# The first two graphs of a pre-norm attention kernel: read by whole rows and turned by the tensor engine, with the first products made one graph at a time

## The chip, the cores and the metric

The kernel runs on one core of a Trainium2 chip. Its time is the device time of one execution in microseconds (us); of five executions the median is 2914.31 us (2913.82 to 2919.03). The profile is of one more execution. Its engines are called PE (tensor engine, matmuls), PEld (its weight loads), DVE (vector), ACT (scalar), POOL (GpSimd) and SP (which here only issues transfers). "ACTq" and "SPq" are transfers being issued by ACT and SP.

## The reference

128 graphs of 128 nodes with 768 features each, all in float32. Each graph is normalised, goes through one attention layer of 12 heads of 64, masked by its adjacency, and the result is added to the input.

```python
h = jnp.maximum(_layernorm(x, axis=-1), 0.0)          # x: (128, 128, 768)
q, k, v = (split_heads(h @ W + b) for W, b in ((Wq, bq), (Wk, bk), (Wv, bv)))
scores = einsum('bhqd,bhkd->bhqk', q, k) / sqrt(64) + beta * adj[:, None]
scores = where(adj[:, None] > 0, scores, -9e15)
out = x + merge_heads(einsum('bhqk,bhkd->bhqd', softmax(scores), v))
```

## The kernel before, in words

**Groups and slices.** The graphs are taken in 32 groups of four (`NG` = 32). The projection of a group is cut into three slices of the weights: `qk0` (q and k of heads 0 to 5), `v`, and `qk1` (q and k of heads 6 to 11). A slice is a product of a 2 x 3 block matrix A and a 3 x 3 block matrix B. A is the group's normalised input, transposed: block `A{r}{k}` has graphs 2r and 2r+1 (256 columns) and features of chunk k (two sub-blocks of 128). B is the slice's weights, nine blocks of 128 x 2 x 256.

**Two ways of making a slice.** `slice_of` makes it with 15 products instead of 18 (`PRODUCTS`), from sums of blocks of A (`SUMS_A`, 11 DVE adds, line 285) and of B (`SUMS_B`, 15 DVE adds, lines 204 and 207); each product is 4 matmuls, each issued in two halves of 64 columns (line 331). The very first slice, `qk0` of group 0, is made by `plain_slice` (line 466): 6 outputs (r, j), each the sum over k of A{r}{k} times B{k}{j}, so 18 products of 4 matmuls of 256 columns (line 477), which need no sums. A finished output is copied from its PSUM bank by ACT with the bias added (line 484). The `v` and `qk1` slices of group 0 are already made with sums, and the weights of `qk0` are summed for group 1. `sum_weights` overwrites some raw blocks (`HOME`).

**The start.** `load_x` reads a graph with four transfers of 96 KB, one for each quarter of the features, 32 nodes to 32 partitions, so that 32 x 32 block transposes on DVE (line 279) finish the transpose. As a node's features then lie on four partitions, its mean and variance need a sum across partitions: `stats` (DVE, line 227), `moments_1` and `moments_2` (small matmuls with `mean8`, lines 238 and 254, and short DVE operations), a power on POOL (line 261), and `norm` on ACT (line 272), before `to_hT` transposes. Four graphs are loaded first, on the SP and ACT queues in turn (line 154), then the weights of `qk0` on SP, and `beta` and two biases on ACT (lines 211, 216, 217). `half(0, ...)` (line 498) makes the A blocks of graphs 0 and 1; `half(1, ...)` those of graphs 2 and 3, with its moments placed after steps 1 and 2 of the plain slice. Ten matmuls on the identity (line 526) run between the moments and the first product.

**What sets the order.** Each engine runs its instructions in order. A scheduler orders them from the order of the code; `tc.issue_after` holds an instruction back behind another. Extra work is hung on the steps of a slice (`then(n, f)`, run after product n). Transfers share eight completion semaphores in turn, so a transfer is issued only when the one eight before it in the code has landed, and everything behind it on its queue waits, ACT's arithmetic included.

**Further on in group 0.** During the `v` slice DVE takes the statistics of group 1 and the sums of `qk1`; at the end of it `bias_1` and `bias_2` prepare the mask of group 0 (DVE lines 298 to 304, ACT line 305, DVE line 310). Scores of heads 0 to 5 (line 377, `scores(0, 0)`) are made behind the second product of `qk1`; they take six PSUM banks, which DVE frees one by one when it adds the mask (line 381, tile `e`). The same happens with `scores(0, 1)` behind the second product of group 1.

The first matmuls of the plain slice:

```python
for k in range(3):
    a, b = A[G, f"A{r}{k}"], wt[sl, f"B{k}{j}"]
    for i in range(2):
        for c in range(2):
            nc.tensor.matmul(p[:, i, :], b[:, c, i * P:(i + 1) * P], a[:, c, :], ...)
```

Of the kernel before, what the change touches and what calls it, by code (L numbers as in the profile page):

```python
# [10 lines left out]
F32 = mybir.dt.float32  # L11
# [6 lines left out]
P = 128  # L18
HEADS = 12
GRP = 4  # L20
# [74 lines left out]


HOME = {"B00": "T12", "B10": "T10", "B02": "T0", "B20": "T4", "B11": "T13"}
SLICES = ("qk0", "v", "qk1")


SC_AT = 1
AV_AT = (5, 8, 11)

LAST = (0, 1, 2, 3, 5, 7, 6, 10, 11, 9, 4, 12, 8, 13, 14)

# [6 lines left out]
def direct(ctx, tc, x, adj, wq, bq, wk, bk, wv, bv, beta, out, bad):  # L112
# [35 lines left out]
    def load_x(G, g, engines):  # L148
        t = xg[G, g] = work.tile([P, NB, QD], F32, tag="x", name=f"x_{G}_{g}")
        src = x[G * GRP + g].rearrange("(b i) (a f) -> a i b f", i=SQ, a=NB)  # L150
        for a in range(NB):
            engines[a % len(engines)].dma_start(t[a * SQ:(a + 1) * SQ], src[a])  # L152

    for g in range(GRP):
        load_x(0, g, (nc.sync, nc.scalar))
    ident = const.tile([P, P], F32, name="ident")
    make_identity(nc, ident)


    fold = const.tile([P, SQ], F32, name="fold")  # L160
    nc.vector.tensor_reduce(fold, ident.rearrange("p (a i) -> p i a", i=SQ), AX.X, ALU.add)
    mean8 = const.tile([P, NB, SQ], F32, name="mean8")
    made = nc.vector.tensor_scalar(mean8, fold[:, None, :].to_broadcast([P, NB, SQ]), -0.125, None, op0=ALU.mult)
    nhalf = const.tile([P, 1], F32, name="nhalf")
    nc.gpsimd.memset(nhalf, -0.5)
    ones = const.tile([P, 1], F32, name="ones")
# [4 lines left out]
    seen_b = const.tile([P, GRP], F32, name="seen_b")  # L171
    nc.gpsimd.memset(seen_b, 0.0)
    vring = [const.tile([P, 2 * GRP, VE], F32, name=f"v{i}") for i in range(7)]
    for v in vring:
        nc.gpsimd.memset(v[:, :, HD:VE], 1.0)
    nv = [0]


# [10 lines left out]
            for i, w in enumerate((wq, wk)):  # L189
                nc.sync.dma_start(t[:, :, i * P:(i + 1) * P], part(w, oc * P, P))  # L190

    def load_weights(sl):
        for b in [f"B{k}{j}" for j in range(3) for k in range(3)]:
            t = const.tile([P, 2, H2], F32, name=f"{sl}_{HOME.get(b, b)}")
            load_block(sl, int(b[1]), int(b[2]), t)
            wt[sl, b] = t
# [9 lines left out]
        else:  # L206
            nc.vector.tensor_tensor(wt[sl, name], wt[sl, a], wt[sl, b], ALU.add if sign > 0 else ALU.subtract)

    load_weights("qk0")
    beta_c = const.tile([P, 1], F32, name="beta_c")  # L210
    nc.scalar.dma_start(beta_c, beta[None, :].to_broadcast([P, 1]))

    nc.gpsimd.tensor_scalar(beta_c, beta_c, ISCALE, None, op0=ALU.mult)
    bqk = const.tile([P, 2, NC], F32, name="bqk")
    with nc.allow_non_contiguous_dma(reason="two biases of one row each"):
        nc.scalar.dma_start(bqk[:, 0, :], bq.rearrange("(c p) -> p c", p=P))
# [5 lines left out]
    def stats(G, g):  # L222

        if G not in st:
            st[G] = stat.tile([P, GRP * NB, nc.vector.BN_STATS_DIM], F32, tag="st", name=f"st_{G}", bufs=2)
        for b in range(NB):
            nc.vector.bn_stats(st[G][:, g * NB + b, :], xg[G, g][:, b, :])  # L227
# [4 lines left out]
    def moments_1(G, lo, hi):  # L232

        n = hi - lo
        bank = pm[G, lo, "bank"] = take()
        pm[G, lo] = bank[:, 0:4 * n].rearrange("p (s b h) -> p s b h", s=2, h=2)
        for q in range(0, P, HD):
            nc.tensor.matmul(pm[G, lo][q:q + HD, 0], mean8.rearrange("p a i -> p (a i)")[:, q:q + HD],
                             halves(G, lo, hi, 1), start=True, stop=True)
        mean = stat.tile([P, n], F32, tag="mean", name=f"mean_{G}_{lo}", bufs=2)  # L240
        nc.vector.tensor_reduce(mean, pm[G, lo][:, 0], AX.X, ALU.add)
        d = stat.tile([P, n, 2], F32, tag="dev", name=f"dev_{G}_{lo}", bufs=2)
        nc.vector.tensor_tensor(d, halves(G, lo, hi, 1), mean[:, :, None].to_broadcast([P, n, 2]), ALU.add)
        nc.vector.tensor_tensor(d, d, d, ALU.mult)
        nc.vector.scalar_tensor_tensor(d, halves(G, lo, hi, 2), 2.0 / QD, d, op0=ALU.mult, op1=ALU.add)
        return mean, d

    squares = {}

    def moments_2(G, lo, hi, mean, d):  # L250

        n = hi - lo
        for q in range(0, P, HD):
            squares[0] = nc.tensor.matmul(pm[G, lo][q:q + HD, 1], mean8.rearrange("p a i -> p (a i)")[:, q:q + HD],
                                          d, start=True, stop=True)
        ve = stat.tile([P, n], F32, tag="ve", name=f"ve_{G}_{lo}", bufs=2)
        nc.vector.tensor_reduce(ve, pm[G, lo][:, 1], AX.X, ALU.add)
        give(pm[G, lo, "bank"])
        nc.vector.tensor_scalar(ve, ve, -1.0, EPS, op0=ALU.mult, op1=ALU.add)
        r = stat.tile([P, n], F32, tag="rstd", name=f"rstd_{G}_{lo}", bufs=2)  # L260
        nc.gpsimd.tensor_tensor(r, ve, nhalf.to_broadcast([P, n]), ALU.pow)  # L261
        t = stat.tile([P, n], F32, tag="shift", name=f"shift_{G}_{lo}", bufs=2)
        shifted = nc.gpsimd.tensor_tensor(t, mean, r, ALU.mult)  # L263
        for b in range(lo, hi):
            rstd[G, b], shift[G, b] = r[:, b - lo:b - lo + 1], t[:, b - lo:b - lo + 1]
        return shifted

    def norm(G, g):
        for b in range(NB):
            t = xg[G, g][:, b, :]  # L270
            n = g * NB + b
            nc.scalar.activation(t, t, AF.Relu, bias=shift[G, n], scale=rstd[G, n])  # L272
# [193 lines left out]
    def plain_slice(G, sl, todo):  # L466

        n = 0
        for r in range(2):
            for j in range(3):  # L470
                bank = take()
                p = bank.rearrange("p (i w) -> p i w", i=2)
                for k in range(3):
                    a, b = A[G, f"A{r}{k}"], wt[sl, f"B{k}{j}"]
                    for i in range(2):
                        for c in range(2):
                            nc.tensor.matmul(p[:, i, :], b[:, c, i * P:(i + 1) * P], a[:, c, :],  # L477
                                             start=(k == 0 and i == 0 and c == 0), stop=(c == 1),
                                             skip_group_check=True)
                    if k == 2:  # L480
                        t = qk[G, sl, r, j] = work.tile([P, 2, H2], F32, tag="qk", name=f"{sl}_{G}_{r}_{j}", bufs=8)
                        oc = j + 3 * int(sl[2])
                        for i in range(2):
                            nc.scalar.activation(t[:, i, :], p[:, i, :], AF.Identity, bias=bqk[:, i, oc:oc + 1])
                        give(bank)
                    for f in todo.get(n, ()):
                        f()
                    n += 1
# [1 line left out]

    adj_0 = load_adj(0)
    nc.sync.dma_start(bv_b, bv[None, :].to_broadcast([P, D]))
    load_weights("v")

    PARTS = (((0, NB), (NB, 2 * NB)), ((2 * NB, 4 * NB),))
    first = {}

    def half(r, step):
        for lo, hi in PARTS[r]:
            graphs = range(lo // NB, hi // NB)  # L500
            if step == 0:
                for g in graphs:
                    stats(0, g)
            elif step == 1:
                first[lo] = moments_1(0, lo, hi)
            else:
                first["pool"] = moments_2(0, lo, hi, *first[lo])
                for g in graphs:
                    norm(0, g)
        if step == 2:  # L510
            for k in range(3):
                first["dve"] = to_hT(0, r, k)

    def after(f, *args):

        with tc.issue_after(first["dve"].ins), tc.issue_after(first["pool"].ins):
            return f(*args)

    with tc.issue_after(made.ins):
        for step in range(3):  # L520
            half(0, step)

    with tc.issue_after(squares[0].ins):
        warm = take()
        for n in range(10):
            nc.tensor.matmul(warm[:, 0:P], ident, ident, start=True, stop=True)
        give(warm)

    def behind_adds(f, *args):

        with tc.issue_after(added[0].ins):
            return f(*args)

    for G in range(NG):
        todo = attention(G - 1, 1) if G else {}

        def then(n, f):
            todo.setdefault(n, []).append(f)
# [7 lines left out]
                if G:  # L546
                    then(11 + g, lambda g=g: stats(G + 1, g))
        if not G:
            load_weights("qk1")
            with tc.issue_after(first["dve"].ins):  # L550
                half(1, 0)
            then(1, lambda: half(1, 1))
            then(2, lambda: half(1, 2))
            for n in range(len(SUMS_A)):
                then(n + 5, lambda n=n: after(sum_acts, 0, n))
            for n in range(len(SUMS_B)):
                then(n // 2 + 5, lambda n=n: after(sum_weights, "v", n))
            plain_slice(0, "qk0", todo)
        else:
            if G == 1:  # L560
                for n in range(8, len(SUMS_B)):
                    then(n - 8, lambda n=n: sum_weights("qk0", n))
            slice_of(G, "qk0", todo)
        todo = {SC_AT: [lambda: scores(G, 0)]} if G else {}
        if G + 1 < NG:
# [188 lines left out]
```

## Time and profile before

| | us |
|---|---|
| median of five executions | 2914.31 |
| their range | 2913.82 to 2919.03 |
| the profiled execution | 2915.2 |
| its span, first to last instruction | 2913.4 |
| PE busy in the span | 2885.1 (99%) |
| DVE / ACT / POOL busy | 1993.4 / 796.1 / 375.6 |
| first matmul of the plain slice (line 477) | 15.56 |
| first product of the `v` slice (line 331) | 49.37 |

A row of a timeline gives the start, the duration, the engine, the line, what is written and read, the shape and the count, and in brackets how long the engine had been idle and what ended that. PE records a float32 matmul as two entries, so "x8" is one product of four matmuls of 256 columns. In a table by stretches, the column behind the busy times is the granted clock of PE as a share of full speed.

### The profile page before, as it was taken

How to read it: one execution, taken by the hardware profiler on the slowest of the kernel's cores; microseconds unless marked ns; L12 is line 12 of the kernel's file. 1: busy time of each engine (PE TensorE's matmuls, PEld its weight loads, DVE VectorE, ACT ScalarE, POOL GpSimd, SP SyncE). 2: the span in 40 equal slices, each digit the busy share in tenths (PEclk: the TensorE clock that was granted, in tenths of full speed). 3: DMA queues.
4: the chain of work that ended last, by engine and by line, in shares of the span. 5: the costliest groups of instructions: out<-in, count | busy, mean ns of one | idle time of the engine just before them, and what ended most of it. 6: DMA issues, size and time to landing. Idle time of an engine off the chain costs nothing.

```text
span 2913.4 us, 81848 instructions
## 1 busy us (share of the span) xinstructions
PE 2885.1 (99%) x35526; PEld 2022.2 (69%) x35526; DVE 1993.4 (68%) x5155; ACT 796.1 (27%) x1703; POOL 375.6 (13%) x307
## 2 busy tenths in 40 slices
PE   8999999999999999999999999999999999999998
PEld 6666676766767667766677666677667776666766
DVE  7866676766767666767667676677766677666765
ACT  1322222323223232222222232322323222222221
POOL 1111111111111111111111111111111111111110
PEclk9999999999999999999999999999999999999999
DMA  5211122111221212222112212122121222111211
GB/s 162 69 56 45 53 70 65 52 54 44 67 70 52 58 42 61 71 59 56 45 52 70 67 50 55 45 67 70 53 62 37 61 70 59 56 45 49 67 41 38
DMA packets 358622, 172.22 MB, mean 59 GB/s; under 512 B 84464, under 2 KB 358128, under 8 KB 358256
## 3 DMA queue, kind: packets, MB, share of 16 engines
q1 hardware_dynamic: 355392, 166.14, 20.8%
q8 instruction: 280, 4.59, 0.6%
q10 hardware_dynamic: 2864, 0.79, 0.1%
q14 instruction: 86, 0.70, 0.1%
HBM read 116.53 MB, written 50.33 MB: 57 GB/s over the span
## 4 chain that ended last, share of the span: by engine, by line
PE 81%; issue 9%; DVE 5%; POOL 2%; DMA 2%; SPq 1%; ACT 0%; ACTq 0%; POOLq 0%; DVEq 0%
PE bank L331 70%; PE bank L377 5%; PE bank L406 5%; DMA x<-in_x_dram 2%; PE bank L477 1%; POOL rstd L261 1%; DVE S L285 1%; POOL xo L411 1%; DVE qk L356 1%; DVE st L227 1%; DVE A L279 1%; DVE o L392 0%; SPq L152 0%; ACT x L272 0%; DVE v L342 0%
## 5 line engine op out<-in xcount | busy, mean ns | idle before, releaser
L331 PE MATMUL bank<-S,qk_T 128*64 128x256 f32 x7056 | 828.7, 382 | 10.5 <-DVE e L381 8.9
L331 PEld LDWEIGHTS bank<-S,qk_T 128*64 128x64 f32 x7056 | 506.0, 138 | 271.1 <-DVE e L381 13.1
L356 DVE TENSOR_TENSOR qk<-qk,bank 128x512 f32<-128x512 f32 x630 | 430.0, 683 | 348.8 <-PE bank L331 348.4
L352 ACT ACTIVATE qk<-bank,bqk 128x256 f32<-128x256 f32 x756 | 313.0, 470 | 1014.2 <-PE bank L331 859.3
L331 PE MATMUL bank<-A,qk_T 128*64 128x256 f32 x4032 | 478.7, 379 | 0.0
L331 PE MATMUL bank<-S,qk_B 128*64 128x256 f32 x4032 | 478.4, 380 | 0.0
L411 POOL TENSOR_TENSOR xo<-xo,o 128x512 f32<-128x512 f32 x189 | 255.8, 1354 | 1611.1 <-DVE o L392 1030.4
L331 PE MATMUL bank<-v_T,S 128*64 128x256 f32 x3584 | 422.9, 381 | 0.0
L384 ACT ACTIVATE e<-e 128x512 f32<-128x512 f32 x378 | 227.5, 631 | 679.7 <-DVE e L381 679.2
L347 DVE TENSOR_TENSOR v<-v,bank 128x512 f32<-128x512 f32 x320 | 220.0, 688 | 264.8 <-PE bank L331 264.8
L331 PEld LDWEIGHTS bank<-A,qk_T 128*64 128x64 f32 x4032 | 284.2, 137 | 136.5 <-issue 0.2
L331 PEld LDWEIGHTS bank<-S,qk_B 128*64 128x64 f32 x4032 | 278.4, 137 | 127.9 <-DVE qk L356 0.8
L331 PEld LDWEIGHTS bank<-v_T,S 128*64 128x64 f32 x3584 | 252.8, 137 | 125.8 <-issue 5.7
L272 ACT ACTIVATE x<-x,shift,rstd 128x192 f32<-128x192 f32 x512 | 228.0, 533 | 343.7 <-POOL shift L263 343.7
L331 PE MATMUL bank<-v_B,S 128*64 128x256 f32 x2048 | 244.8, 380 | 0.0
L381 DVE SCALAR_TENSOR_TENSOR e<-bank,biasT 128x512 f32<-128x512 f32 x378 | 231.4, 680 | 13.6 <-PE bank L377 13.5
L331 PE MATMUL bank<-v_T,A 128*64 128x256 f32 x2048 | 238.4, 379 | 0.0
L342 DVE TENSOR_TENSOR v<-bv_b,bank 128x512 f32<-128x512 f32 x192 | 131.8, 687 | 145.8 <-PE bank L331 145.8
L406 PEld LDWEIGHTS bank<-v,e 128*64 128x64 f32 x6048 | 208.6, 138 | 27.4
L279 DVE STREAM_TRANSPOSE A<-x 128x256 f32<-128x256 f32 x384 | 215.7, 613 | 7.5 <-ACT x L272 7.4
L227 DVE BATCH_NORM_STATS2 st<-x 128x6 f32<-128x192 f32 x512 | 160.5, 348 | 71.6 <-DMA x<-in_x_dram 71.4
L406 PE MATMUL bank<-v,e 128*64 128x65 f32 x6048 | 208.4, 221 | 0.0
(79 smaller groups left out, 1726.6 us busy)
## 6 DMA issues: line engine op xcount, KB each, us to landing
x<-in_x_dram SPq DMA_DIRECT2D x504, 96.0 KB, 2.3
xo<-in_x_dram SPq DMA_DIRECT2D x189, 256.0 KB, 2.8
out_dram<-xo SPq DMA_DIRECT2D x189, 256.0 KB, 2.2
adj<-in_adj_dram SPq DMA_DIRECT2D x128, 64.0 KB, 2.3
qk_T<-in_L_gnn_Wq_dram SPq DMA_DIRECT2D x10, 128.0 KB, 3.3
qk_T<-in_L_gnn_Wk_dram SPq DMA_DIRECT2D x10, 128.0 KB, 3.1
v_T<-in_L_gnn_Wv_dram SPq DMA_DIRECT2D x5, 256.0 KB, 5.9
qk_B<-in_L_gnn_Wq_dram SPq DMA_DIRECT2D x8, 128.0 KB, 3.0
```

Of the source, the lines that this page charges most:

```text
L227: nc.vector.bn_stats(st[G][:, g * NB + b, :], xg[G, g][:, b, :])
L272: nc.scalar.activation(t, t, AF.Relu, bias=shift[G, n], scale=rstd[G, n])
L279: last = nc.vector.transpose(t[:, :, g * N:(g + 1) * N].rearrange("p c (b i) -> p c b i", i=SQ), src)
L331: nc.tensor.matmul(p[q:q + HD, i, :], lhs[:, q:q + HD], rhs, start=(first and i == 0 and c == 0), stop=(c == 1), skip_group_check=True)
L347: added[G] = nc.vector.tensor_tensor(o, o, got, ALU.add if sign > 0 else ALU.subtract)
L352: nc.scalar.activation(t[:, i, :], p[:, i, :], AF.Identity, bias=bqk[:, i, oc:oc + 1], scale=float(sign))
L356: added[G] = nc.vector.tensor_tensor(t, t, p, ALU.add if sign > 0 else ALU.subtract)
L377: nc.tensor.matmul(ps[oc, i][k:k + HD, g * N:(g + 1) * N], t[r, 1, at][:, k:k + HD], t[r, 0, at], start=True, stop=True)
L381: nc.vector.scalar_tensor_tensor(e, ps[oc, i].rearrange("p (g n) -> p g n", g=GRP), SCORE_CAP * ISCALE, biasT[G], op0=ALU.min, op1=ALU.add)
L384: nc.scalar.activation(e, e, AF.Exp, scale=1.0 / ISCALE)
L406: nc.tensor.matmul(pa[q:q + HD, 2 * g + i, :], es[G, oc, i][:, 2 * r + g, q:q + HD], vt[G, "v", r, h // 4][:, 4 * g + h % 4, :], start=Tru ...
L411: nc.gpsimd.tensor_add(t, t, o.rearrange("p a (b j) d -> p (a b) (j d)", j=2))
```

## The change

Graphs 0 and 1 are read by whole rows: a node's 768 features on one partition, with two transfers of 64 rows (192 KB) for each graph, one on SP and one on ACT. `rows_1` gets mean and variance of a row with two statistics operations, one that combines them, an addition and a power on POOL. `rows_2` normalises, three chunks of 256 features (graph 0 on DVE, graph 1 on ACT), transposes each 128 x 128 on PE, and applies the ReLU while copying out of PSUM (graph 0 on ACT, graph 1 on DVE, the other way about). Graphs 2 and 3 keep the old way.

Output (0, 0) of the plain slice is made graph by graph: 12 matmuls of 128 columns for graph 0, then 12 for graph 1, in place of 12 of 256.

Around it: the first three weight blocks (`B00`, `B10`, `B20`) are read before graphs 2 and 3; eight matmuls on the identity run as soon as it is there; the moments of graphs 2 and 3 come after steps 3 and 4 instead of 1 and 2; the blocks of `v` and `qk1` are read in the order in which the sums need them (`AS_SUMMED`); the last seven sums of `qk0` wait for an addition of group 0's `v` slice (`behind_adds`); `mean8`, the scaling of `beta` and the filling of the `v` tiles come later in the code.

```diff
+AS_SUMMED = ("B01", "B12", "B02", "B22", "B10", "B00", "B21", "B20", "B11")
+WARM = 8
...
-    for g in range(GRP):
-        load_x(0, g, (nc.sync, nc.scalar))
+    for g in range(2):
+        t = xg[0, g] = work.tile([P, NB, QD], F32, tag="x", name=f"x_0_{g}")
+        for h, engine in enumerate((nc.sync, nc.scalar)):
+            rows = slice(h * HD, (h + 1) * HD)
+            engine.dma_start(t[rows].rearrange("p b f -> p (b f)"), x[g, rows])
...
-    load_weights("qk0")
+    load_weights("qk0", ["B00", "B10", "B20"])
+    for g in range(2, GRP):
+        load_x(0, g, (nc.sync, nc.scalar))
+    load_weights("qk0", [f"B{k}{j}" for j in range(1, 3) for k in range(3)])
...
-                for k in range(3):
+                parts = (slice(0, N), slice(N, H2)) if r == j == 0 else (slice(0, H2),)
+                for at, k in [(at, k) for at in parts for k in range(3)]:
...
-                            nc.tensor.matmul(p[:, i, :], b[:, c, i * P:(i + 1) * P], a[:, c, :],
+                            nc.tensor.matmul(p[:, i, at], b[:, c, i * P:(i + 1) * P], a[:, c, at],
...
-    load_weights("v")
+    load_weights("v", AS_SUMMED)
...
+    def rows_1(g):
+        t = xg[0, g].rearrange("p b f -> p (b f)")
+        s = stat.tile([P, 2, nc.vector.BN_STATS_DIM], F32, tag="strow", name=f"strow_{g}", bufs=2)
+        for h in range(2):
+            nc.vector.bn_stats(s[:, h, :], t[:, h * VH:(h + 1) * VH])
+        mv = stat.tile([P, nc.vector.BN_AGGR_DIM], F32, tag="mvrow", name=f"mvrow_{g}", bufs=2)
+        nc.vector.bn_aggr(mv, s)
+        ve = stat.tile([P, 1], F32, tag="verow", name=f"verow_{g}", bufs=2)
+        nc.vector.tensor_scalar(ve, mv[:, 1:2], EPS, None, op0=ALU.add)
+        r = stat.tile([P, 1], F32, tag="rsrow", name=f"rsrow_{g}", bufs=2)
+        nc.gpsimd.tensor_tensor(r, ve, nhalf, ALU.pow)
+        return mv, r
+
+    def rows_2(g, mv, r):
+        v = xg[0, g].rearrange("p b (j c) -> p c (b j)", c=NC)
+        if g:
+            sh = stat.tile([P, 1], F32, tag="shrow", name="shrow", bufs=1)
+            nc.vector.scalar_tensor_tensor(sh, mv[:, 0:1], -1.0, r, op0=ALU.mult, op1=ALU.mult)
+        for k in range(3):
+            n = work.tile([P, 2, P], F32, tag="e", name=f"rows_{g}_{k}", bufs=6)
+            if g:
+                with tc.issue_after(first["act"].ins):
+                    nc.scalar.activation(n, v[:, 2 * k:2 * k + 2], AF.Identity, bias=sh, scale=r)
+            else:
+                nc.vector.tensor_scalar(n, v[:, 2 * k:2 * k + 2], mv[:, 0:1], r, op0=ALU.subtract, op1=ALU.mult)
+            bank = take()
+            p = bank[:, 0:H2].rearrange("p (c i) -> p c i", c=2)
+            for c in range(2):
+                nc.tensor.transpose(p[:, c, :], n[:, c, :], ident)
...
+            if g:
+                first["dve"] = nc.vector.tensor_scalar(t, p, 0.0, None, op0=ALU.max)
+            else:
+                first["act"] = nc.scalar.activation(t, p, AF.Relu)
+            give(bank)
...
+    for n in range(WARM):
+        nc.tensor.matmul(warm[:, 0:P], ident, ident, start=True, stop=True)
...
-            load_weights("qk1")
+            load_weights("qk1", AS_SUMMED)
...
-            then(1, lambda: half(1, 1))
-            then(2, lambda: half(1, 2))
+            then(3, lambda: half(1))
+            then(4, lambda: half(2))
...
-                    then(n - 8, lambda n=n: sum_weights("qk0", n))
+                    then(n - 8, lambda n=n: behind_adds(sum_weights, "qk0", n))
```

## The prediction

> **What bounds the kernel now.** I began with the page's busy times, then read PE's timeline of the first 180 us, the granted clock there, and the timelines of DVE, ACT and POOL for what ends PE's gaps.
>
> ```profile
> PE 2885.1 (99%) x35526; PEld 2022.2 (69%) x35526; DVE 1993.4 (68%) x5155; ACT 796.1 (27%) x1703; POOL 375.6 (13%) x307
> ```
>
> PE is idle for 28.3 us in all. Whatever starts the first product earlier is won only if PE's later gaps don't swallow it. PE's timeline (start, duration, what ended the idle time):
>
> ```profile
> 9.23 4.42 PE L526 MATMUL bank<-ident 128*128 128x128 f32 x20
> 15.56 5.41 PE L477 MATMUL bank<-A,qk_T 128*128 128x256 f32 x16 [1.91 <-DVE A L279]
> ...
> 23.27 2.00 PE L477 MATMUL bank<-A,qk_B 128*128 128x256 f32 x8
> ...
> 49.37 1.95 PE L331 MATMUL bank<-v_T,S 128*64 128x256 f32 x16
> ...
> 85.75 6.63 PE L331 MATMUL bank<-S,qk_T 128*64 128x256 f32 x32 [3.07 <-DVE e L381]
> ...
> 123.72 6.43 PE L331 MATMUL bank<-S,qk_T 128*64 128x256 f32 x32 [3.31 <-DVE e L381]
> ```
>
> Output (0, 0) occupies 15.56 to 23.27, the plain slice ends at 49.37, and there are two gaps of over 3 us, both ended by DVE's mask addition. After each of the three idle stretches a product takes about twice its usual 1.73 us. The granted clock (fourth number) says why:
>
> ```profile
> 16.50:17.00 0.50, 0.50 (x3) 0.69 0.84 248
> 20.00:20.50 0.50, 0.50 (x3) 0.90 1.22 201
> 84.00:85.00 1.00, 0.00 (x0) 0.98 0.00 0
> 91.00:92.00 1.00, 1.00 (x8) 0.61 0.00 0
> 122.00:123.00 1.00, 0.00 (x0) 0.75 0.05 5
> 129.00:130.00 1.00, 1.00 (x12) 0.83 0.00 0
> ```
>
> From these shares the clock falls to half at 16.69, 84.96 and 122.5 and comes back at 20.10, 91.78 and 129.34: all apart by multiples of 3.41 us. [...] A stretch that was 78% busy (84.96 to 88.37) did not bring it back.
>
> The second gap hangs on one chain, read in the timelines of POOL, ACT and DVE:
>
> ```profile
> 68.77 3.20 POOL L261 TENSOR_TENSOR rstd<-ve,nhalf 128x16 f32<-128x16 f32 x1 [42.95 <-DVE ve L259]
> 72.51 6.25 ACT L272 ACTIVATE x<-x,shift,rstd 128x192 f32<-128x192 f32 x14 [22.20 <-POOL shift L263]
> 78.66 0.61 ACT L305 ACTIVATE adjT<-adjT 128x512 f32<-128x512 f32 x1
> 79.31 0.69 DVE L310 TENSOR_REDUCE bm<-adjT 128x4 f32<-128x512 f32 x1 [3.47 <-ACT adjT L305]
> 85.05 3.63 DVE L381 SCALAR_TENSOR_TENSOR e<-bank,biasT 128x512 f32<-128x512 f32 x6
> 123.00 1.27 DVE L381 SCALAR_TENSOR_TENSOR e<-bank,biasT 128x512 f32<-128x512 f32 x2
> ```
>
> From `bm` at 79.31 to the mask addition at 123.00 DVE waits for PE only once, 0.87 us. So the restart of PE at 123.72, and with it the end, is `bm` plus DVE work, and `bm` is tied to the `v` slice by the moments of group 1. From 130 on DVE has idle time again.
>
> **The change, part by part.**
>
> *When graph 0 can be copied out.* The cross-partition moments go (16 small matmuls, 12 short DVE operations, until 9.72) with 6 stream transposes (0.57 each). In their place: the rows land by about 4.2 and 5.6 (the same bytes landed by 4.4 and 6.2 before). The order of the built kernel puts graph 0's `ve` on DVE behind graph 1's first statistics, so it waits for graph 1's rows too: 5.6 + 0.5 = 6.1. POOL's power took 1.05 us for 4 columns and 1.63 for 8; for one column that line gives 0.6: 6.9. Three normalisations at 0.3 to 0.4 each, two transposes: the first bank is full at about 8.5. But ACT isn't free. Its queue issues transfers first:
>
> ```profile
> 7.02 0.36 ACTq L211 DMA_DIRECT2D beta_c<-in_L_gnn_beta_dram  x1
> ...
> 8.74 0.38 ACTq L217 DMA_DIRECT2D bqk<-in_L_gnn_bk_dram  x1
> 9.29 1.28 ACT L272 ACT_TABLE_LOAD   x1 [9.29 <-DMA qk_T<-in_L_gnn_Wq_dram]
> ```
>
> In the changed order the last of these (`bk`) reuses the semaphore of `beta`, and `beta` that of graph 1's second half. `beta` goes out at 5.6 and takes 3.4 us to land (its row), so `bk` goes at 9.0, the table load runs from 9.6 to 10.9, and the first ReLU (0.47, the row of a 128 x 256 copy) ends at 11.5. Bounds: 10.6 if `beta` lands in 2.5 us (the shortest x landing is 2.4), 12.1 if the rows land as late as 6.2.
>
> *Output (0, 0).* PE goes on from 11.5, not 15.56, but has been idle before, so at half clock. By the rows the clock comes back after 3.41 to 6.82 us of full work; I take 4.9. A matmul of 128 columns: the ten of line 526 took 0.44 each; half of a warm one of 256 columns is 0.215. I take 0.43 at half clock and 0.24 at full. Graph 1's six transposes stand among graph 0's products in PE's order; no row shows one, between 0 and the 0.44 of line 526 I take 0.2. Then 4.9 us hold the transposes (1.2) and 8.6 matmuls, and the other 15.4 take 3.7: output (0, 1) starts at 20.1. Bounds 17.5 (10.6, 3.41 us, 0.215 each, transposes nothing) and 24.5 (12.1, all at half clock at 0.44, transposes 0.3). Before it was 23.27, with both pairs of moments done (0.23 each in PE's starts); they now come later. Gain 23.27 - 20.1 - 0.46 = **2.7 us**, between -1.7 and 5.3.
>
> [...] No run shown here has a transpose on PE.
>
> *Graphs 2 and 3.* Their moments move two products later, against a first product that is earlier. From the second moments (23.04) to block A10 it took until 30.1, 7.1 us. Now between these moments and output (1, 0) stand 0.23 + 4 products of 1.73 = 7.14 us. So A10 comes just in time: 0, bounded by 0 and 0.5. The slack of 3.6 us that was there (30.1 to 33.73) is used up. The weights are no bound: SP issued the last of `qk0` at 16.7, and three semaphore waits put it at the same place.
>
> *DVE before the `v` slice.* The A blocks of graphs 2 and 3 are done at 32.1, 26 sums at 0.60 end at 47.8, statistics (1.13) at 48.9. The `v` slice starts at 49.37 - 2.7 = 46.7, and its first result is there at 48.65. So DVE is 0.3 us late, where it had waited 2.90 us. It had 1.39 us of idle time before `ve` to make it up: 0, at most 0.5. `v` blocks landed by about 31 and are read in the order of use.
>
> *`bm`.* In the built order the Square on ACT stands behind 12 of the 16 normalisations, not 14: 2 x 0.45 = -0.9. `ve` of group 1 stands one addition and one sum later on DVE: +0.5, between 0 and 1.7. Together **-0.4**.
>
> *From `bm` to 123.00.* Counting the DVE list: the same operations but one fewer statistics: **-0.3**. The three `qk0` sums that ran early (two at 19.18, one at 46.72, 1.8 us) now end up among and behind the six mask additions; PE's two half-clock products cover them, then DVE's idle time. Without that cover 0.6 to 1.8.
>
> *Nothing else* on PE's list changes order but by a few matmuls. Sum: -2.7 - 0.4 - 0.3 = -3.4 us. Against the profiled execution (2915.2, span 2913.4) that gives 2911.8 and 2910.0; the median is 0.9 below the profiled one: **2910.9 us**.
>
> **Rivals.**
>
> *A, more is won: 2907.4.* The phase of the 3.41 us stretches is luck. Where the clock comes back early in (0, 0), the start is up to 1.6 us better (18.5); the first DVE gap shrinks to 2.6 us, and if it straddles two stretches the clock stays up and DVE's 0.87 us wait goes; after the second gap half clock may last 3.4 us and not 5.6, worth 1.0. All three: -6.9. For it: the five runs differ by 1.5 us apart from one. Against: they must fall together.
>
> *B, PE stays cold through (0, 0): 2913.8.* Broken by waits for graph 1's copies, no stretch is full; all at half clock (0, 1) starts at 11.5 + 24 x 0.43 + 1.2 = 23.0, with the last few warm at 22.3. The gain of 2.7 becomes 0.2, the sum -0.5. For it: 78% busy wasn't enough.
>
> *C, slower: 2916.8.* A10 comes late. Its place is between outputs (0, 2) and (1, 0), its cause that the moments of graphs 2 and 3 stand two products later and their rows are read behind three weight blocks. If the chain takes 3 us more than 7.1, PE idles for 3 us, the clock falls, and half clock costs another 2.9 (5.7 us at half, as after 85.75): -3.4 + 5.9 = +2.5, and DVE's sums move with it. It decides from about 1.5 us of lateness on. Against: x of graph 3 lands by about 14, and the moments aren't due before 21.
>
> *D, nothing: 2914.3.* ACT's queue is held until about 15, so that the first product starts when it did. Then the rows' early arrival is hidden. It needs `beta` to take 7 us to land.
>
> **How the numbers follow.** The forecast has 0.45, A 0.33, B 0.12, C 0.06, D 0.04. The range of 2905.5 to 2914.5 us takes in A, B, D and the bounds of the start; it leaves out C and the far tail of A. About 0.2% (5.8 us) is what a measurement of this kernel tells from no change. Of A 0.28 lies beyond that, of the forecast's spread 0.10: faster 0.38. Slower by so much only in the worst of C, with 0.03. The rest, 0.59, is within 0.2%.
>
> **What would show it.** In the profile after: the table load at 9.6 and the first L478 matmul near 11.5; half clock for some 5 us from there; (0, 1) near 20; no PE idle time of over 0.5 us before (1, 0); the first `v` product at 46.7; `bm` at 76.2; the restart behind the second gap at 120.3. I am wrong if PE waits in the plain slice for A10 or weights, if the ReLU starts before 10, if DVE reaches the `v` slice more than 1 us late, or if the second gap isn't ended by DVE.

## The result, and the profile after

| | before | after |
|---|---|---|
| median, us (76 and 40 executions) | 2913.16 | 2908.49 |
| range | 2908.28 to 2919.03 | 2904.66 to 2909.65 |
| the profiled execution, its span | 2915.2, 2913.4 | 2906.74, 2905.0 |

The ratio is 0.9984 with a 95% interval of 0.998 to 0.9988: 4.67 us less, where the prediction said 3.4 less. Its forecast of 2910.9 us was 2.4 too high; 1.15 of that is the median of the kernel before, which was 2914.31 ahead of the prediction and is 2913.16 here. The two profiled executions are 8.5 us apart, so one of them or both were unusual, and the first question to a line below is whether it would be the same in another execution.

Busy times, from the page:

```profile
PE 2881.5 (99%) x35542; PEld 2024.2 (70%) x35542; DVE 1987.5 (68%) x5144; ACT 795.1 (27%) x1701; POOL 374.5 (13%) x305
```

PE's timeline (start, duration, what ended the idle time), at the places that were shown of before:

```profile
8.79 1.54 PE L529 MATMUL bank<-ident,rows 128*128 128x128 f32 x6 [2.92 <-DVE rows L525]
11.94 2.50 PE L478 MATMUL bank<-A,qk_T 128*128 128x128 f32 x10 [1.61 <-ACT A L537]
...
16.14 3.96 PE L478 MATMUL bank<-A,qk_T 128*128 128x128 f32 x34
19.94 1.89 PE L478 MATMUL bank<-A,qk_B 128*128 128x256 f32 x8
...
46.79 1.95 PE L330 MATMUL bank<-v_T,S 128*64 128x256 f32 x16
...
82.50 3.67 PE L330 MATMUL bank<-S,qk_T 128*64 128x256 f32 x32 [2.22 <-DVE e L380]
...
117.91 5.36 PE L330 MATMUL bank<-S,qk_T 128*64 128x256 f32 x32 [3.09 <-DVE e L380]
```

Graph 0's chunks are on PE at 8.79 and turned by 10.33, but the first product waits until 11.94 for ACT. Its first five matmuls (ten entries) fill 2.29 us to the next start, 0.46 each; the 17 from 16.14 on fill 3.80, 0.22 each. Both gaps are still there. Behind the first the two products take 3.67 us (6.63 before), so the clock stayed up (1.00 in each row from 80 to 88 us); behind the second they take 5.36. The granted clock (fourth number):

```profile
9.00:9.50 0.50, 0.50 (x4) 0.28 (x2) 0.50 (x2) 0.00 (x0) 0.20 (x1) 0.56 1.03 207
15.50:16.00 0.50, 0.50 (x5) 0.50 (x4) 0.24 (x1) 0.00 (x0) 0.00 (x0) 0.61 1.04 289
118.00:119.00 1.00, 1.00 (x8) 0.57 (x10) 1.00 (x3) 1.00 (x2) 0.00 (x0) 0.64 0.00 0
121.00:122.00 1.00, 1.00 (x8) 0.62 (x6) 1.00 (x3) 0.45 (x1) 0.00 (x0) 0.65 0.00 0
```

By these shares it falls at 9.06 and comes back at 15.89, 6.83 us later; behind the second gap it is down for 3.42 us, 118.28 to 121.70. Why PE waited until 11.94, from ACT's timeline, and the chain to the second gap, from those of POOL, ACT and DVE:

```profile
9.75 0.43 ACTq L218 DMA_DIRECT2D bqk<-in_L_gnn_bk_dram  x1
10.21 1.28 ACT L537 ACT_TABLE_LOAD   x1 [10.21 <-DMA bqk<-in_L_gnn_bq_dram]
11.50 0.94 ACT L537 ACTIVATE A<-bank 128x256 f32<-128x256 f32 x3
```

```profile
66.80 2.91 POOL L260 TENSOR_TENSOR rstd<-ve,nhalf 128x16 f32<-128x16 f32 x1 [40.13 <-DVE ve L258]
70.11 5.37 ACT L271 ACTIVATE x<-x,shift,rstd 128x192 f32<-128x192 f32 x12 [22.37 <-POOL shift L262]
75.39 0.61 ACT L304 ACTIVATE adjT<-adjT 128x512 f32<-128x512 f32 x1
76.03 0.69 DVE L309 TENSOR_REDUCE bm<-adjT 128x4 f32<-128x512 f32 x1 [2.60 <-ACT adjT L304]
81.81 3.63 DVE L380 SCALAR_TENSOR_TENSOR e<-bank,biasT 128x512 f32<-128x512 f32 x6
117.17 1.29 DVE L380 SCALAR_TENSOR_TENSOR e<-bank,biasT 128x512 f32<-128x512 f32 x2
```

| | before | predicted | after |
|---|---|---|---|
| first matmul of the plain slice | 15.56 | 11.5 | 11.94 |
| output (0, 1) | 23.27 | 20.1 | 19.94 |
| first `v` product | 49.37 | 46.7 | 46.79 |
| `bm` of group 0 | 79.31 | 76.2 | 76.03 |
| first mask addition of the second six | 123.00 | | 117.17 |
| restart behind the second gap | 123.72 | 120.3 | 117.91 |
| span | 2913.4 | 2910.0 | 2905.0 |

Up to `bm` the change did what was predicted, within 0.5 us at each place. From `bm` on this execution gained 2.55 us more on DVE, where 0.3 was predicted. DVE's wait of 0.87 us for PE behind the first gap went, since the clock stayed up: luck, as a gap of the same 2.22 us cost 1.7 us in two of the kernels below. One fewer statistics stands there: 0.3. Another 0.3 is spread over many operations. And a sum next to a POOL addition was not held up; DVE's and POOL's rows, first before and then after:

```profile
99.47 2.36 DVE L285 TENSOR_TENSOR S<-A,A 128x512 f32<-128x512 f32 x2
99.56 1.72 POOL L411 TENSOR_TENSOR xo<-xo,o 128x512 f32<-128x512 f32 x1 [27.08 <-DVE o L392]
```

```profile
94.54 1.28 DVE L284 TENSOR_TENSOR S<-A,A 128x512 f32<-128x512 f32 x2
94.63 2.93 POOL L410 TENSOR_TENSOR xo<-xo,o 128x512 f32<-128x512 f32 x1 [24.55 <-DVE o L391]
```

Two sums that take 1.28 us took 2.36 before; after, POOL was the one that lost (2.93 instead of 1.72). In all 12 profiles of the experiments this pair shows 2.36 or 2.37 on DVE and 1.72 or 1.73 on POOL. So the 1.08 us belong to this one execution.

### The profile page after: what moved, and what is told of

It reads as the page before. It is cut to its first block, busy times and chain, and to the rows that moved or that the text cites. A ratio compares the mean times of both kernels' runs of the same rounds, so it can differ in the third digit from the quotient of the medians.

```text
span 2905.0 us, 81845 instructions
## 1 busy us (share of the span) xinstructions
PE 2881.5 (99%) x35542; PEld 2024.2 (70%) x35542; DVE 1987.5 (68%) x5144; ACT 795.1 (27%) x1701; POOL 374.5 (13%) x305
## 4 chain that ended last, share of the span: by engine, by line
PE 86%; issue 6%; DVE 4%; DMA 2%; POOL 1%; SPq 0%; ACT 0%; POOLq 0%; DVEq 0%
PE bank L330 74%; PE bank L376 5%; PE bank L405 5%; DMA x<-in_x_dram 1%; PE bank L478 1%; DVE S L284 1%; DVE qk L355 1%; POOL rstd L260 1%; POOL xo L410 1%; DVE st L228 1%; DVE A L278 1%; DVE qk_T L207 0%; DVE o L391 0%; DVE e L380 0%; DVE v L341 0%
```

## The experiments

The theory after the result: the gain is the earlier start of output (0, 1), carried along one chain (`v` slice, `bm`, DVE's work, mask additions) to the end; the rest of the 8.4 us between the two spans is luck. "Below before" is against executions of the kernel before on the same chip (medians of 2912.4 to 2913.1). Differences between two of the medians below are mostly of kernels on different chips and, at 1 us or less, not clear of noise.

**Output (0, 0) whole again.**

```diff
-parts = (slice(0, N), slice(N, H2)) if r == j == 0 else (slice(0, H2),)
+parts = (slice(0, H2),)
```

> The changed kernel, with output (0, 0) made whole again: 12 matmuls of 256 columns instead of 12 of 128 for graph 0 and 12 for graph 1. Theory (the gain is the earlier start of output (0, 1), 23.27 to 19.94, carried to the end): the first product now needs graph 1's copies, of which the first ended at 15.3 in the profile after; without products between them the transposes move up by about 1, so the first product starts near 14.2, at half clock for 3.4 to 6.8 us, and (0, 1) at 20.4 to 23, about 1.6 later than in the changed kernel. The median is then 3.1 us below the kernel before, where the changed kernel is 4.7 below; the v slice starts near 48.4 instead of 46.8. Rival (the order extras carry the gain, the start is hidden): still 4.7 below, whatever the start does.

2909.66 us, 3.4 below before (ratio 0.999, 0.9981 to 0.9999). PE's timeline shows the wait for graph 1's rows:

```profile
13.24 1.41 PE L529 MATMUL bank<-ident,rows 128*128 128x128 f32 x4 [3.15 <-ACT rows L523]
```

(0, 1) starts at 21.77, the `v` slice at 48.62, `bm` at 78.83, and the Square stands behind 14 normalisations again. The places moved as the theory said, and the median fits it: graph by graph would be worth about 1.2 us of the 4.7. But the interval also takes in the changed kernel's 0.9984, so the median alone does not exclude the rival.

**The order extras undone.**

```diff
-load_weights("v", AS_SUMMED)
+load_weights("v")
-load_weights("qk1", AS_SUMMED)
+load_weights("qk1")
-then(3, lambda: half(1))
-then(4, lambda: half(2))
+then(1, lambda: half(1))
+then(2, lambda: half(2))
-then(n - 8, lambda n=n: behind_adds(sum_weights, "qk0", n))
+then(n - 8, lambda n=n: sum_weights("qk0", n))
```

> The changed kernel with its order extras undone: moments of graphs 2 and 3 after steps 1 and 2, the blocks of v and qk1 read in the plain order, the last seven qk0 sums not held back. Theory: these are worth nothing or little; the moments of graphs 2 and 3 now stand inside output (0, 0), where PE waits for DVE's statistics (they end at 19.3) for up to 0.8 us. The median is 3.9 to 4.7 us below the kernel before. Rival (the extras are a good part of the gain): at most 2.5 us below, with PE or DVE waiting for a transfer of v in the 26 sums, or the first gap of PE longer by the 1.8 us of three sums.

2909.92 us, 3.2 below before (0.9992, 0.9983 to 1.0001): between the two. PE waits 0.70 us for the second moments (21.60) and the `v` slice starts at 47.06. The first gap is as long as in the changed kernel (2.23), the second longer (3.58), with nine statistics between 116.40 and the addition at 119.50. By the medians the extras are worth about 1.4 us together, but this interval, too, takes in 0.9984; which part carries what was not separated.

**ACT's queue free.** SP issues everything but two transfers; the two biases are moved like `beta`.

```diff
-load_x(0, g, (nc.sync, nc.scalar))
+load_x(0, g, (nc.sync,))
-nc.scalar.dma_start(beta_c, beta[None, :].to_broadcast([P, 1]))
+nc.sync.dma_start(beta_c, beta[None, :].to_broadcast([P, 1]))
```

> The changed kernel with the transfers of graphs 2 and 3, beta and the two biases issued by SP alone, so that ACT's queue holds nothing but two transfers of graph 0 and 1 before the ReLU. Theory (the start is held by ACT's queue, not by the rows): the table load is done before 8, the first ReLU starts when its bank is full, near 9.3, the first product at 9.7 instead of 11.94, output (0, 1) at about 17.6 instead of 19.94, and the median is another 2.3 us lower, 7.0 below the kernel before. If the rows of graph 3 or the biases now land too late, up to 1.5 of this is lost. Rival (PE's earlier start is swallowed by DVE, which was already the last to be ready at the v slice): no lower than the changed kernel, with PE waiting for DVE's sums or additions before or in the v slice.

2905.47 us, 7.6 below before (0.9978, 0.9968 to 0.9987). ACT's timeline in that kernel:

```profile
1.97 1.28 ACT L537 ACT_TABLE_LOAD   x1 [1.97 <-issue]
8.96 0.81 ACT L537 ACTIVATE A<-bank 128x256 f32<-128x256 f32 x2 [5.71 <-PE bank L529]
```

The table is loaded early, the ReLU waits for PE alone, the first product starts at 9.77, (0, 1) at 17.93, the `v` slice at 45.14. Step "ACT isn't free" of the prediction is shown: ACT's transfers held the start, by 2.2 us. The scheduler also put the Square in front of all normalisations here (`bm` at 71.17, the normalisations from 73.84), and the first mask addition comes at 79.69 instead of 81.81. How much of the 3 us below the changed kernel is the start and how much this order was not separated.

**The mask of group 0 earlier.**

```diff
-then(10, lambda: bias_2(0, behind_adds(bias_1, 0, adj_0)))
+then(4, lambda: first.update(a=behind_adds(bias_1, 0, adj_0)))
+then(10, lambda: bias_2(0, first["a"]))
```

> The changed kernel with the mask of group 0 prepared after step 4 of the v slice instead of step 10, so that the Square and bm no longer stand behind 12 normalisations on ACT. Theory (both gaps of PE are set by the chain bm, DVE work, mask addition): DVE's wait of 2.60 us before bm goes, the first mask addition moves from 81.81 to about 79, PE's first gap of 2.22 us shrinks to under 0.5, the second restart moves from 117.91 to about 115, and the median is 2.2 to 2.9 us below that of the changed kernel, about 7.2 below the kernel before. Rival (the gaps follow from the scores or from DVE's total work, not from bm): the wait only moves elsewhere on DVE, and the median stays 4.7 below the kernel before, within 0.7.

2906.64 us, 6.5 below before (0.9979, 0.997 to 0.9988). The wait before `bm` is gone, the first mask addition comes at 79.01, the first gap vanishes and the second restart is at 115.81, all near the places that the theory gave. The median is 1.9 below the changed kernel, a little less than the 2.2 to 2.9 expected, and the second gap is as long as ever, 3.08 us.

**The sums behind the second mask additions.** `behind_masks` holds an instruction back behind the last of the second six.

```diff
-then(n - 8, lambda n=n: behind_adds(sum_weights, "qk0", n))
+then(n - 6, lambda n=n: behind_masks(sum_weights, "qk0", n))
```

> The changed kernel with the last seven qk0 sums held behind the second six mask additions (those of scores(0, 1)). In the profile after, four of these sums (2.4 us) stand on DVE between 114.11 and the first mask addition at 117.17. Theory (the second gap of PE, 3.09 us, is DVE work ahead of that addition): it comes at about 114.8, when its scores are there, PE restarts at about 115.5 instead of 117.91, and the gap is about 0.7. That is 2.4 us, and up to 1.7 more if the clock stays up over so short a gap: the median is 2.4 to 4.1 us below that of the changed kernel, 7.1 to 8.8 below the kernel before. Rival (work on DVE can only be moved, PE waits for it a little later, for the sums or for the mask of group 1): under 1 us below the changed kernel, with new waits of PE between 120 and 150.

2907.70 us, 5.0 below before (0.9985, 0.9976 to 0.9994): the rival's figure. DVE's timeline shows that the place was taken:

```profile
114.51 0.87 DVE L228 BATCH_NORM_STATS2 st<-x 128x6 f32<-128x192 f32 x3
115.38 0.69 DVE L309 TENSOR_REDUCE bm<-adjT 128x4 f32<-128x512 f32 x1
115.98 0.35 DVE L228 BATCH_NORM_STATS2 st<-x 128x6 f32<-128x192 f32 x1
116.25 0.14 DVE L310 TENSOR_TENSOR seen_b<-seen_b,bm 128x4 f32<-128x4 f32 x1
116.31 1.13 DVE L228 BATCH_NORM_STATS2 st<-x 128x6 f32<-128x192 f32 x4
117.36 1.27 DVE L380 SCALAR_TENSOR_TENSOR e<-bank,biasT 128x512 f32<-128x512 f32 x2
```

Eight statistics of group 2, which nobody needs so early, stand where the four sums stood. No new wait of PE appears, so it is not that DVE lacks slack later.

**Three edits together** (ACT's queue, the mask, the sums).

> The changed kernel with three edits at once: ACT's queue free of transfers, the mask of group 0 after step 4 of the v slice, and the last seven qk0 sums behind the second mask additions. Alone, the first two were 3.0 and 1.9 us below the median of the changed kernel (2905.47 and 2906.64 against 2908.49). Theory (start, first gap and second gap are three separate losses in one chain): they add up, with 2.4 to 4.1 for the third: 7.3 to 9.0 us below the changed kernel, 12 to 13.7 below the kernel before. Rival (DVE's total work from the v slice to the second mask addition sets the time once its waits are gone): PE waits for DVE in the v slice or at the gaps for what the earlier start won, and the sum is at most 5 us below the changed kernel.

2905.45 us, 7.3 below before (0.9978, 0.9969 to 0.9987), no better than ACT's queue alone. The theory of separate losses falls: the mask's operations, now in front of `ve` (70.42), delay ACT's normalisations to 74.29, DVE waits 1.38 and 1.11 us for them with two transposes that stand ahead of the first mask addition (80.14), and the second addition is again behind eight statistics (116.28). The kernel with only ACT's queue free had most of the mask in front of `ve` (70.36) already, and DVE waits of 0.21 and 1.11 us, so the second edit had little left to win.

**A longer start on the identity** (on top of ACT's queue: `WARM = 13`).

> The kernel with ACT's queue free of transfers, with 13 instead of 8 matmuls on the identity at the start, so that PE is busy from 2.2 until graph 0's transposes at 8.2 and from there on. Without them the first ten entries of the first product took 2.34 us and the next ones became fast only at about 14. Theory (the clock follows PE's busy time in the 3.41 us stretch before): two such stretches after 2.2 is 9.0 at the latest, so the first product starts at full clock near 9.8, ten entries take 1.2 us, output (0, 1) starts at about 15.8 instead of 17.93, and the median is 2.0 us lower, at 2903.5. If block A10 or DVE's sums then come late, PE waits before (1, 0) or the v slice for up to what was won. Rival (the pause of 2.3 us at 6 was not what kept the clock down): the entries take as long as before, and the median is within 0.5 us of 2905.5.

2905.84 us, 6.9 below before (0.9979, 0.997 to 0.9988): the rival's figure, but not for its reason. In PE's timeline the matmuls end early, and a pause follows:

```profile
2.19 4.78 PE L543 MATMUL bank<-ident 128*128 128x128 f32 x26 [2.19 <-POOL ident masks.py:199]
8.82 1.74 PE L529 MATMUL bank<-ident,rows 128*128 128x128 f32 x6 [1.86 <-DVE rows L525]
10.35 2.27 PE L478 MATMUL bank<-A,qk_T 128*128 128x128 f32 x10
```

26 entries took 4.78 us, where 16 take 3.78 (0.24 each, 6.1 for 26); a row of 0.5 us holds four or five of them up to 5.5, then six and seven, so by the durations the clock came up on the way. In the 3.41 us up to 9.0 PE was then busy for only 1.55, and the granted clock was 0.50 from 9.0 to 12.42. So the longer start did not keep the clock up for the first product. This profile, and the next one, are of the slowest of their eleven executions (2908.82 and 2908.88 us).

**The same with transposes.** 26 transposes of the identity instead.

> As the kernel with 13 matmuls on the identity, but with 26 transposes of the identity in their place, which fill the same time on PE as single entries. Theory (transposes count as work for the clock, as the profile after suggests, where two pairs stood in the stretch from 12.47 to 15.89 and the clock came back at its end): the same start, output (0, 1) at about 15.8. [...]

2906.27 us, 6.5 below before (0.9978, 0.9969 to 0.9987). PE's timeline:

```profile
2.18 5.73 PE L543 MATMUL bank<-ident 128*128 128x128 f32 x26 [2.18 <-POOL ident masks.py:199]
8.78 0.87 PE L529 MATMUL bank<-ident,rows 128*128 128x128 f32 x4 [0.87 <-DVE rows L525]
9.84 0.44 PE L529 MATMUL bank<-ident,rows 128*128 128x128 f32 x2 [0.18 <-DVE shrow L518]
10.11 1.28 PE L478 MATMUL bank<-A,qk_T 128*128 128x128 f32 x10
```

Nothing but transposes ran on PE before 10.11, and the first ten entries take 1.28 us, where they took 2.27 in the kernel with 13 matmuls: by the durations the clock was up at 10.11. (0, 1) starts at 17.03 and the `v` slice at 43.89, 1.25 earlier than with ACT's queue alone (45.14), but the second mask addition comes at 115.90 against 115.67, and the median does not follow. In this kernel the Square stands behind three normalisations again, DVE waits 2.88 us for it ahead of `bm` (73.54), and the first mask addition gains only 0.36 us on the kernel with ACT's queue alone: DVE's list and what it waits for, not PE, set it.

**Sums and statistics behind the second mask additions** (on the changed kernel; the line below is for group 1, where it holds the statistics of group 2).

```diff
-then(11 + g, lambda g=g: stats(G + 1, g))
+then(11 + g, lambda g=g: behind_masks(stats, 2, g))
```

> The changed kernel with not only the last seven qk0 sums but also the 16 statistics of group 2 held behind the second six mask additions. With the sums alone held, the scheduler had put eight statistics (114.51 to 117.36, 2.4 us) in their place, eight more stood earlier, and the mask addition came at 117.36 as before. Theory (the second gap is whatever DVE work is let in front of that addition): 4.5 us of work goes, so the first addition follows its scores, near 113.8 to 114.5, and PE restarts by 115.8 with a gap under 0.7, against 118.09 and 2.76. The median is 2.3 to 4 us below that with the sums alone (2907.7): 2903.7 to 2905.4. Rival (DVE has no slack to take it later): PE waits between 120 and 160 for sums, moments or the mask of group 1, and the median is within 1 us of 2907.7.

2902.64 us, 9.7 below before (0.9967, 0.9954 to 0.9979) and 5.9 below the changed kernel. PE's timeline, the scores and what follows:

```profile
112.23 2.85 PE L376 MATMUL bank<-qk 64*64 64x128 f32 x96
115.01 3.67 PE L330 MATMUL bank<-S,qk_T 128*64 128x256 f32 x32
```

The second gap is gone and no new one appears: it was work that DVE did too early.

**Only that hold, on the kernel before.**

> The kernel before, with only the hold: the last seven qk0 sums and the 16 statistics of group 2 behind the second six mask additions, as in the changed kernel with both held (2902.64). The start is the old one. Theory (the change's gain is the earlier start, and it stays whole when the second gap is gone): the second gap of 3.31 us and its half clock go, 5 to 7 us below the kernel before, and what is left between this and 2902.64 is the gain of the start, 2.7 to 4.7 us: 2905.3 to 2907.3. Rival (the change's gain was mainly what it did to the second gap, in which fewer statistics and sums stood): this kernel comes within 1.5 us of 2902.64.

2907.22 us, 5.6 below before (0.9981, 0.9972 to 0.999). The difference to the last kernel is the change alone, with no second gap in either: 4.58 us between the medians, 4.1 when each is taken against the kernel before on its own chip. Either is the 4.67 of the change within noise, so the gain does not come from the second gap, and the rival falls. PE's timeline, the first two products and the restart behind the scores:

```profile
15.62 3.72 PE L477 MATMUL bank<-A,qk_T 128*128 128x256 f32 x16 [1.68 <-DVE A L279]
...
117.44 3.67 PE L331 MATMUL bank<-S,qk_T 128*64 128x256 f32 x32
```

At the restart the two profiled executions are 2.43 us apart (117.44 and 115.01), at the end 4.0. The start is the old one, but its first two products run at full clock (3.72 us; 5.41 in the profile of before, where the clock fell at 16.69), and (0, 1) starts at 21.64 instead of 23.27. So with the old start, too, (0, 1) came at times that are 1.6 us apart.

**All of it:** ACT's queue, the mask, sums and statistics, and the first transposes of group 1 behind the first six mask additions.

```diff
-with tc.issue_after(added[G].ins):
+with tc.issue_after(added[G].ins), tc.issue_after((added[G] if G else added[0, 0]).ins):
...
-then(at, lambda n=n: transposes(n))
+then(at if G else max(at, SC_AT), lambda n=n: transposes(n))
```

> ACT's queue free of transfers, the mask of group 0 after step 4 of the v slice, the first transposes of group 1 held behind the first six mask additions, and the last qk0 sums and the statistics of group 2 behind the second six. In the kernel with three of these edits the first addition waited until 80.14 for transposes whose input ACT had not normalised, and the second until 116.28 behind eight statistics. Theory (each gap is the DVE work let in front of its mask addition): the first addition follows its scores at about 76.6, PE's first gap is under 0.7 (restart near 78.8 instead of 80.40 in the kernel with only ACT's queue freed), the second restart is near 112 instead of 116.41, and the median is 4 to 6 us below that kernel's 2905.5, so 2899.5 to 2901.5. Rival (the start and the gaps cannot be won together, since DVE's work from the v slice on has no slack): new waits of PE for DVE behind the gaps, and a median not below 2904.

2901.34 us, 11.0 below before (0.9965, 0.9952 to 0.9979), the lowest median of the case. The first addition comes at 76.77 and the second at 113.30. But PE, going on at 78.41, stops after one product:

```profile
83.42 0.87 PE L330 MATMUL bank<-S,qk_T 128*64 128x256 f32 x6 [3.06 <-ACT qk L351]
```

ACT copies the first two products of `qk1` only after 16 normalisations.

**The last eight normalisations behind those copies.**

> The kernel with all five edits (2901.34), with the last eight normalisations of group 1 on ACT placed behind the copies of the first two qk1 products. There PE's first gap had ended early, at its mask additions, but PE then waited 3.06 us (until 83.42) for those copies, which stood behind 16 normalisations; DVE waited 1.60 for the same. Theory (this wait is the price of the late moments): it goes, of which 1.6 to 3 us are kept, as DVE's list up to the second mask addition moves by its 1.60 at least: 2898.3 to 2899.8, with the second gap growing from 0.40 by up to 1.4. Rival (the normalisations are only late elsewhere): the transposes of group 1 wait for ACT instead, and the median is within 0.7 us of 2901.34.

2902.67 us, 10.2 below before (0.9966, 0.9954 to 0.9978). The wait of 3.06 is gone (PE goes on without a pause at 79.01), and still the median is no lower. It is 1.3 above the last kernel, just outside the rival's 0.7; the two sets of five and six executions overlap, so no difference between them is shown. PE now waits 0.55, 0.44 and 0.45 us for DVE's additions, and the second mask addition comes at 113.00, only 0.30 earlier. This looks like the reason seen with the transposes of the identity: DVE's list from the `v` slice to the second mask addition is the bound, and PE's head start is only lent. Holding work back from that list gave the largest gain above (9.7 us below before); what else on it could wait was not tried.

## Why the prediction was right

*When graph 0 can be copied out.* Right in mechanism, 0.4 us optimistic in size. The rows landed at 4.88 and 6.81 instead of 4.2 and 5.6, `bk` went out at 9.75 instead of 9.0. That ACT's queue is the holder was tested by emptying it.

*Output (0, 0).* 20.1 predicted, 19.94 measured, from errors that cancel: a later start, and 3.95 us at half clock instead of 4.9. From one start to the next, a matmul of 128 columns took 0.43 at half clock (14.66 to 15.09), as taken; the first five, with the start-up of the first, took 0.46 each. At full clock it took 0.22 (0.24 taken). A pair of transposes took 0.43 at half clock (14.23 to 14.66) and 0.22 at full (15.92 to 16.14), so 0.2 for one was right at half clock and twice too much at full. The clock's bounds were rightly set, and they matter: it came back at 15.89 here, and by the durations between 14.6 and 15.2 in the kernel with the extras undone.

*Transposes and the clock.* The forecast took the transposes for work like any other, and that was right here: the clock came up at 15.89, with two pairs of them in the 3.41 us before, and in the kernel with 26 transposes it was up at 10.11 behind nothing else. The runs show at which times the clock changed; what decides that, on which A and the kernel with 13 matmuls rest suppositions, they do not show. (Two slips in the prediction's reading change nothing: the 16 small matmuls are 16 entries, that is 8 matmuls, and the stretch called 78% busy was 77%.)

*Graphs 2 and 3.* (1, 0) starts without a wait, as counted. *DVE before the `v` slice:* its first addition comes at 48.79 without waiting, a little late, and nothing follows from it.

*`bm`.* -3.28 measured against -3.1. The Square does stand behind 12 normalisations. `ve` was 1.90 earlier where 2.2 was counted.

*From `bm` to 123.00.* The step that was too small: -0.3 predicted, -2.55 in this execution, of which 0.87 (the clock that stayed up) and 1.08 (POOL's place beside a sum) are luck and 0.3 is the missing statistics.

*The sum.* -3.4 against -4.67. Without the luck behind `bm`, the steps of this pair make -3.6: 2.58 to the `v` slice, 0.7 to `bm`, 0.3 behind it. The 0.7 is the same in the kernels that keep these starts (29.93 and 29.94 us from the `v` slice to `bm` with the old one, 29.24 with the new one, three times). The 2.58 is not: with the old start the `v` slice began at 49.37 and 47.74, with the new one at 46.79, 47.12, 46.22 and 45.98, so that pairs of these are 0.6 to 3.4 apart, 2.0 in the mean. That it came so near the predicted 2.7 is in part luck. More of the gain may lie in PE's short waits between 130 and the last group: 4.0 us in the profile of before, 2.6 in that of after, and again 4.0 and 2.6 in the two kernels with the second gap closed. With the 2.0 and this 1.4 the sum would be 4.4. But the ten other profiles with the new start show 2.6 to 5.3 (seven of them under 3.6), and why they are mostly shorter was not tried, so the last 1 us or so of the 4.67 stays open.

*Rivals.* A, the luck of the phases, took place in the profiled execution in two of its three parts, but the median, 1.75 us above that execution, does not have all of it. A's 2907.4 is nearer to the measured 2908.49 than the forecast is; against the kernel before as measured with it, the forecast's -3.4 is nearer to -4.67 than A's -6.9. B, C and D did not happen; D's mechanism, ACT's queue, was there with 2.2 us, not all 4.

## What to carry to other kernels

Here a transfer on ACT's queue that waited for a completion semaphore (`bk`, until 9.75) held ACT's arithmetic, and with it the first product by 2.2 us; look there first when data have landed and nothing starts. Where a gap is ended by an engine with much deferrable work, ask what its scheduler would put in the place of what you take away, and hold all of it. And the head start was worth no more than the next engine's list allowed: emptying ACT's queue gave 3 us, another 1.2 us of start gave nothing that could be measured.

## What the runs showed of the hardware

*A gap's price was luck.* Of 21 gaps of 2.0 to 3.6 us ended by mask additions in 12 profiles, 5 cost no clock (the next two products took 3.67 us, one of these gaps 2.99 long), 14 cost 1.35 to 1.7 (5.02 to 5.36) and 2 cost 2.8 to 3.0. 1.7 us is half of the 3.42 us for which the clock was down behind the second gap of the changed kernel. A gap of 2.22 us cost 1.7 in two kernels and nothing in a third.

*The clock's column started at 1.00 whatever the clock was.* In the kernel with 13 matmuls it reads 1.00 from 2 to 9.0, while a row of 0.5 us holds four entries at 2.5, as at half clock, and seven at 6.0; only from the first recorded change on (9.0 there) was it to be trusted. Before that, durations tell.

*POOL and DVE held each other up.* At this one place a 128 x 512 sum on DVE beside a POOL addition of the same size took about 1.76 us (2.36 less the 0.60 of the first of the pair) instead of 0.68 in 13 of 14 profiles. In the profiles of before and after every other such sum kept its 0.6 to 0.7 us, those beside a POOL addition too.
